# Putting the second layer's first row fetches ahead of its loads in GpSimd's queue

## The chip, the cores and the metric

The kernel runs on one core of one Trainium2 chip. The metric is the device time of one execution in microseconds (us). Before the change it is 1780.5 us, the median of three runs (1777.8 to 1781.71).

## The reference

A graph of 6250 nodes with 128 features, 50,000 undirected edges (so 100,000 directed ones) and one self-loop for each node, sorted by destination. Two residual layers:

```python
h = relu(layernorm(x))
xw = h @ W                                    # layer 0: a normalised graph convolution
x = x + relu(segment_sum(xw[src] * (dinv[src] * dinv[dst])[:, None], dst) + b)
h = relu(layernorm(x))
q, k, v = h[src] @ Wq.T + bq, h[dst] @ Wk.T + bk, h[dst] @ Wv.T + bv   # layer 1: attention over edges
e = exp(clip(einsum("ehd,ehd->eh", q, k) / 4, -10, 10))                # 8 heads of 16
out = segment_sum(e / (segment_sum(e, src)[src] + 1e-8) * v, src) + h
x = x + layernorm(out) * gamma + beta
```

## The kernel before

Nodes lie in 49 blocks of 128. Layer 0 (`layer0`) walks over the edges in the order of their destination: GpSimd fetches rows of xw from a table in HBM (`gtab`) with indirect DMAs of 128 rows (`gather`, line 397), TensorE adds them up by destination with one-hot matrices, and `finish0` finishes a block of 128 nodes as soon as its last edge is in. Its results go by SyncE's queue to tables in HBM: `htab`, `xtab`, `owntab` (q of each node), `kvtab` (k and v, float32), `qtab` (q as three bfloat16 parts), and, for the first 18 blocks alone, `kvptab` (k and v as three bfloat16 parts). Beside this work the kernel sorts the edges for layer 1: each block of 128 source nodes gets J = 20 tiles of 128 edge places. The first 9 tiles (`CELLS`) hold edges whose other end is in the first 18 blocks (two blocks a tile), the remaining 11 (`FAR`) hold the others in ascending order of that end. `unpack` writes the row numbers to `idx1`, and `rows_of` the lane numbers to `lrow` and `drow`. `flags` adds up checks that all hold, and only then the fast path `layer1` is taken (a branch on `self.flag`, line 1552); else `general` computes everything in another way.

Layer 1 (`layer1`) goes through the 49 blocks in five steps of four tiles each, in the order of tiles [8..11], [0..3], [12..15], [4..7], [16..19]. `fetch` gets k and v of the edges' far ends. For tiles from 9 on, GpSimd gathers rows of `kvtab` into a buffer `kv` (nine of them). For tiles under 9, TensorE multiplies one-hot matrices `ohD` with `kvp`, the copy of `kvptab` that is kept in SBUF for the whole layer: 18 blocks, 3456 KB. The one-hot matrices `ohT` and `ohD` are made by VectorE from the rows `lr` and `dr`, and q of the edges comes from `qb`. `load` brings lr, dr and qb of a block, those of block 0 by GpSimd's queue and the others by SyncE's. `weigh` (two steps later) makes the attention weights, `gather_up` (four steps later) sums up. Every eight blocks, `own_edges` loads hs, x, qo and kvo by SyncE's queue and works out the self-loops.

The order within an engine's queue is the program's order of issue with some freedom for a scheduler that looks at dependences; GpSimd's queue keeps the order written in the source. A buffer of layer 1 that lies where layer 0 had buffers waits until layer 0 has let go of them. GpSimd's queue at the seam between the layers holds, in this order: the last gathers of `gtab`, the read of the flag, the load of kvp (line 978), the loads of lr, dr and qb (lines 1004, 1007, 1009), and the gathers of layer 1.

Of the kernel before, what the change touches and what calls it, by code (L numbers as in the profile page):

```python
# [7 lines left out]
F32 = mybir.dt.float32  # L8
# [6 lines left out]
OP = mybir.AluOpType  # L15
# [6 lines left out]
P = 128  # L22
D = 128
# [5 lines left out]
PB = 18  # L29
CELLS = -(-PB // 2)  # L30
FAR = 11
J = CELLS + FAR
BANK0 = 10
G1 = 4
# [5 lines left out]
CW = -(-P // CN)  # L40
CQ = 4
CR = 8
CL = 8
RUN = 128
SEG = 4
# [7 lines left out]
class Kernel:  # L53
    def __init__(self, ctx, tc, x, srcp, dstp, srct, dstt, bases, firsts, wins, w0, b0, wq, bq, wk, bk, wv, bv,
                 gamma, beta, out, E):
        self.ctx, self.tc, self.nc = ctx, tc, tc.nc
        self.x, self.srcp, self.dstp, self.srct, self.dstt = x, srcp, dstp, srct, dstt
        self.bases, self.firsts, self.wins = bases, firsts, wins
        self.w0, self.b0, self.gamma, self.beta, self.out, self.E = w0, b0, gamma, beta, out, E
        self.qkv = ((wq, bq), (wk, bk), (wv, bv))  # L60
        self.N = x.shape[0]
        self.NB = -(-self.N // P)
        self.NP = self.NB * P
        self.LAST = self.N - (self.NB - 1) * P
        self.EC = -(-E // P)
        self.ER = -(-self.EC // P) * P
        self.NR = -(-E // self.ER)
        self.NG0 = -(-self.EC // G0)
        self.ET = self.NG0 * G0
        self.NT1 = self.NB * J  # L70
        assert self.N <= 8192 and self.EC <= 1024 and self.ER <= 1024 and self.ER % SEG == 0
        assert PB < self.NB <= 49 and BANK0 * self.NB <= 512 and (J - BANK0) * self.NB <= 512

        self.NODE0 = (PC - 1) * P
        self.GA = int(PC * P * E / self.N - 4.5 * (PC * P * (E / self.N - 1)) ** 0.5) // (P * G0)

        self.done_at = {}
        for b in range(PC, self.NB):
            last = b + 1 == self.NB
            self.done_at[b] = self.NG0 - 1 if last else min(self.NG0 - 1, -(-(b + 1) * P * E // (self.N * P * G0)) + 1)  # L80
        self.NW = PC // CQ
        assert PC % CQ == 0 and CN * self.NB * 2 <= 512


# [103 lines left out]
    def head(self):  # L188
        nc, tc, const, NB, NP, N, ER = self.nc, self.tc, self.const, self.NB, self.NP, self.N, self.ER
        d_i = self.rows["dst"]  # L190
        self.flag = const.tile([1, 1], I32, name="flag")

        self.bad = const.tile([P, 7], F32, name="bad")
        nc.vector.memset(self.bad, 0.0)
        self.dinv = const.tile([P, NB], F32, name="dinv")
        self.gtab = self.dram.tile([NP, D], F32, name="gtab")
# [2 lines left out]
        with self.first_c:  # L199
# [3 lines left out]
            bad = self.bad  # L203
# [5 lines left out]
            for g, n in groups(NB, 8):  # L209
                st = hw.tile([P, 8, nc.vector.BN_STATS_DIM], F32, name="st0")  # L210
                for b in range(g, g + n):
# [5 lines left out]
                                               op0=OP.mult, op1=OP.mult)  # L217
# [183 lines left out]
    def layer0(self):  # L401
# [19 lines left out]
        with ExitStack() as l0c:  # L421
# [248 lines left out]
            def unpack():  # L670
                vi = big("vi", I32, "big0", NB * J).rearrange("p (a b) -> p a b", b=J)
                for h, f0, f1 in ((0, 0, BANK0), (1, BANK0, J)):
                    v = pp[:, h, :(f1 - f0) * NB].rearrange("p (j b) -> p b j", b=NB)
                    nc.vector.tensor_scalar(vi[:, :, f0:f1], v, 1024.0, None, op0=OP.mult)
                bv = big("bv", F32, "big1", NB * J).rearrange("p (a b) -> p a b", b=J)
                nc.vector.tensor_scalar(bv, vi, 0.0, None, op0=OP.is_gt, op1=OP.add, accum_out=self.bad[:, 5:6])
                ai = ti(NB * J).rearrange("p (a b) -> p a b", b=J)
                nc.vector.tensor_scalar(ai, vi, 10, None, op0=OP.arith_shift_right)
                bi = bv.bitcast(I32)
                nc.vector.tensor_scalar(bi, vi, 1023, None, op0=OP.bitwise_and)  # L680
                nc.vector.tensor_scalar(idx1, ai, 7, 10, op0=OP.bitwise_and, op1=OP.logical_shift_left)
                nc.vector.tensor_tensor(idx1, idx1, bi, op=OP.bitwise_or)
                nc.vector.tensor_scalar(ai, ai, 3, None, op0=OP.arith_shift_right)
                loc = big("loc", F32, "big2", NB * J).rearrange("p (a b) -> p a b", b=J)
                nc.vector.tensor_scalar(loc, ai, -1.0, None, op0=OP.add)
                r["loc"] = loc.rearrange("p a b -> p (a b)")

                r["rel"] = bv.rearrange("p a b -> p (a b)")[:, :NB * CELLS]
                rel = r["rel"].rearrange("p (a b) -> p a b", b=CELLS)
                nc.vector.scalar_tensor_tensor(rel, self.slot_f[:, None, :CELLS].to_broadcast([P, NB, CELLS]),  # L690
                                               -2.0 * P, idx1[:, :, :CELLS], op0=OP.mult, op1=OP.add)


            def flags():
                p5, k = bank()
                nc.tensor.matmul(p5[:1, :7], self.onef, self.bad, start=True, stop=True)
                want = l0k.tile([1, 7], F32, name="want")
                nc.vector.memset(want, 0.0)
                nc.vector.memset(want[:, 1:4], float(N))
                nc.vector.memset(want[:, 5:6], float(E - N))  # L700
                sums = l0k.tile([1, 7], F32, name="sums")
                nc.vector.tensor_tensor(sums, p5[:1, :7], want, op=OP.not_equal)
                let_go(k)
                fails = l0k.tile([1, 5], F32, name="fails")
                nc.vector.tensor_reduce(fails[:, 0:1], sums, axis=AX.X, op=OP.add)
                bf = l0k.tile([1, self.NG0 + 1], F32, name="bf")
                nc.vector.tensor_copy(bf, base_i)

                wide = l0k.tile([1, self.NG0 - GA], F32, name="wide")
                nc.vector.tensor_sub(wide, bf[:, GA + 1:], bf[:, GA:self.NG0])  # L710
                nc.vector.tensor_scalar(wide, wide, float(WIN - 1), None, op0=OP.is_gt, op1=OP.add,
                                        accum_out=fails[:, 1:2])

                nc.vector.tensor_scalar(fails[:, 3:4], bf[:, GA:GA + 1], float(PC * P), None, op0=OP.is_ge)
                nc.vector.tensor_scalar(fails[:, 4:5], bf[:, GA:GA + 1], float(NODE0), None, op0=OP.is_lt)
                late = l0k.tile([1, NB], F32, name="late")
                nc.vector.memset(late, 0.0)
                for b, at in self.done_at.items():
                    if at + 1 < self.NG0:
                        nc.vector.tensor_scalar(late[:, b:b + 1], bf[:, at + 1:at + 2], float((b + 1) * P), None,  # L720
                                                op0=OP.is_lt)
                nc.vector.tensor_reduce(fails[:, 2:3], late, axis=AX.X, op=OP.add)
                total = l0k.tile([1, 1], F32, name="total")
                nc.vector.tensor_reduce(total, fails, axis=AX.X, op=OP.add)
                nc.vector.tensor_scalar(self.flag, total, 0.0, None, op0=OP.is_equal)
# [240 lines left out]
    def layer1(self):  # L966
# [7 lines left out]
        with ExitStack() as l1c:  # L974
            l1k = l1c.enter_context(tc.tile_pool(name="l1k", bufs=1))
            kvp = l1k.tile([P, PB, 3, 2 * D], BF16, name="kvp")

            nc.gpsimd.dma_start(kvp.rearrange("p b c f -> p b (c f)"),
                                self.kvptab.rearrange("(b p) f -> p b f", p=P))
            l1 = l1c.enter_context(tc.tile_pool(name="l1", bufs=2))  # L980
            pqp = l1c.enter_context(tc.tile_pool(name="pqp", bufs=3, space=PSUM))
            kvps = l1c.enter_context(tc.tile_pool(name="kvps", bufs=2, space=PSUM))
# [18 lines left out]
            def load(b, by=nc.sync):  # L1001
                lr = l1.tile([P, J * P], BF16, name="lr", bufs=3)
                src = self.lrow[b * J:(b + 1) * J, :]
                by.dma_start(lr, bass.AP(tensor=src.tensor, offset=src.offset, ap=[[0, P], [1, J * P]]))
                dr = l1.tile([P, CELLS * P], BF16, name="dr", bufs=2)
                src = self.drow[b * CELLS:(b + 1) * CELLS, :]
                by.dma_start(dr, bass.AP(tensor=src.tensor, offset=src.offset, ap=[[0, P], [1, CELLS * P]]))
                qb = l1.tile([P, 3 * D], BF16, name="qb", bufs=3)
                by.dma_start(qb, qtab_v[:, b, :])
                blocks[b] = [lr, qb, dr]  # L1010


            def fetch(b, k):
                if k == 0 and b + 1 < NB:
# [7 lines left out]
                nc.vector.tensor_scalar(ohT[:, :n * P], lr[:, j0 * P:(j0 + n) * P], pid[:, 0:1], None,  # L1022
                                        op0=OP.is_equal)
                if m < n:
                    kv = l1.tile([P, G1, 2 * D], F32, name="kv", bufs=9)
                    for i in range(m, n):
                        self.gather(kv[:, i, :], self.kvtab, idx1, b * J + tiles[i])
                else:
                    kv = l1.tile([P, G1, 2 * D], F32, name="kvn", bufs=5)
                if m:  # L1030
# [86 lines left out]
                                     mine[:, :cn, D:, None].to_broadcast([P, cn, H, HD]))  # L1117

            own, ends = iter(()), {}
            load(0, nc.gpsimd)  # L1120
            for i in range(len(units) + 4):
                if i < len(units):
# [480 lines left out]
```

## Time and profile before

| what | value |
|---|---|
| median of three runs | 1780.5 us (1777.8 to 1781.71) |
| profiled execution | 2244.92 us, span 2243.1 us |
| busy: TensorE, its weight loads, VectorE | 1672.5, 1427.7, 1512.1 us |
| busy: ScalarE, GpSimd | 967.6, 1143.1 us |
| gathers of `gtab` in layer 0 | 567, 1064 ns each on GpSimd |
| gathers of `kvtab` in layer 1 | 539, 983 ns each on GpSimd |
| GpSimd's DMA queue (q0) | 45264 packets, 112.89 MB |
| SyncE's DMA queue (q1) | 116391 packets, 106.65 MB |
| kvp load | one DMA of 3456 KB |

The profile is of one execution, which was longer than the undisturbed ones; durations are taken from it, and the sum is set against its own time. PE is TensorE, PEld its weight load, DVE VectorE, ACT ScalarE, POOL GpSimd; SPq, POOLq are the queues' DMA issues. In the timeline a line has the start in us, the duration in us, engine, source line, operation, what is written and read, how many merged, and in brackets the idle time of the engine before it with what ended it. In the windows, each engine has its busy time in the stretch.

### The profile page before, as it was taken

How to read it: one execution, taken by the hardware profiler on the slowest of the kernel's cores; microseconds unless marked ns; L12 is line 12 of the kernel's file. 1: busy time of each engine (PE TensorE's matmuls, PEld its weight loads, DVE VectorE, ACT ScalarE, POOL GpSimd, SP SyncE). 2: the span in 40 equal slices, each digit the busy share in tenths (PEclk: the TensorE clock that was granted, in tenths of full speed). 3: DMA queues.
4: the chain of work that ended last, by engine and by line, in shares of the span. 5: the costliest groups of instructions: out<-in, count | busy, mean ns of one | idle time of the engine just before them, and what ended most of it. 6: DMA issues, size and time to landing. Idle time of an engine off the chain costs nothing.

```text
span 2243.1 us, 41246 instructions
## 1 busy us (share of the span) xinstructions
PE 1672.5 (75%) x14772; PEld 1427.7 (64%) x14772; DVE 1512.1 (67%) x4504; ACT 967.6 (43%) x2499; POOL 1143.1 (51%) x1124
## 2 busy tenths in 40 slices
PE   4334687777678888887428888787988888888786
PEld 4333576666566677555317777686877777777676
DVE  7821498768748888998227668566767567556667
ACT  6641544423347767775103334233334334333333
POOL 0565523444647667777465555454555453544540
PEclk9556698888775556998559999888888888999898
DMA  4411222222222222222475335434435333432430
GB/s 93 108 49 48 70 70 77 81 72 73 76 69 71 61 63 64 65 64 64 134 243 162 115 123 156 125 122 149 135 115 164 108 119 107 145 105 95 141 105 13
DMA packets 168217, 225.46 MB, mean 101 GB/s; under 512 B 30026, under 2 KB 127803, under 8 KB 168003
## 3 DMA queue, kind: packets, MB, share of 16 engines
q0 software_dynamic: 45264, 112.89, 17.0%
q1 hardware_dynamic: 116391, 106.65, 15.3%
q10 hardware_dynamic: 6348, 3.20, 0.7%
q8 instruction: 118, 1.93, 0.4%
q14 instruction: 96, 0.79, 0.1%
HBM read 191.42 MB, written 31.20 MB: 99 GB/s over the span
## 4 chain that ended last, share of the span: by engine, by line
PE 58%; issue 15%; DVE 11%; ACT 8%; another core or an unknown queue 3%; DMA 2%; POOL 1%; SPq 1%; DVEq 0%; ACTq 0%; POOLq 0%
PE pk L1040 14%; PE po L1079 11%; PE pq L1048 8%; PE cb L797 7%; PE ps L956 5%; PE pp L658 5%; ACT ola L643 3%; PE ot L1052 3%; PE cb L782 1%; PE ps_f L892 1%; ACT counts L785 1%; DVE oh_tau L645 1%; DVE win_oh L771 1%; POOL gt L397 1%
## 5 line engine op out<-in xcount | busy, mean ns | idle before, releaser
L397 POOL DMA_INDIRECT gt<-gtab,idx x567 | 603.5, 1064 | 484.3 <-issue 140.2
L397 POOL DMA_INDIRECT kv<-kvtab,idx x539 | 530.1, 983 | 526.7 <-issue 141.5
L1040 PE MATMUL pk<-kvp,ohD 128*128 128x256 bf16 x2646 | 368.0, 290 | 77.8 <-issue 67.7
L1040 PEld LDWEIGHTS <-ohD 128*128 128x128 bf16 x2646 | 271.0, 104 | 147.1 <-issue 104.3
L643 ACT ACTIVATE ola<-ol,a_f 128x128 f16<-128x128 f16 x624 | 270.2, 519 | 57.5 <-DVE ol L624 37.7
L1048 PE MATMUL pq<-qb,ohT 128*128 128x128 bf16 x2940 | 237.8, 231 | 57.9 <-issue 57.5
L1054 ACT COPY oh<-ot 128x512 f32<-128x512 f32 x245 | 142.6, 583 | 263.9 <-PE pk L1040 90.3
L956 PE MATMUL ps<-oh,gt 128*128 128x64 f32 x1134 | 214.1, 344 | 56.2 <-DVE acc L938 25.2
L1048 PEld LDWEIGHTS <-ohT 128*128 128x128 bf16 x2940 | 204.9, 104 | 79.8 <-issue 71.3
L956 PEld LDWEIGHTS ps<-oh,gt 128*128 128x128 f32 x1134 | 201.4, 261 | 65.5 <-issue 34.9
L797 PE MATMUL cb<-xwp,counts 128*128 128x128 bf16 x2352 | 192.5, 253 | 51.5 <-issue 39.5
L797 PEld LDWEIGHTS <-counts 128*128 128x128 bf16 x2352 | 185.9, 155 | 60.9 <-issue 48.1
L1060 DVE TENSOR_TENSOR pr<-pq,kv 128x512 f32<-128x512 f32 x147 | 101.0, 687 | 173.9 <-DMA kv<-kvtab,idx 66.0
L658 PE MATMUL pp<-oh_tau,ol 128*128 128x49 f16 (+5 forms) x916 | 192.0, 265 | 28.2 <-DVE ol L626 16.3
L785 ACT CAST counts<-cb 128x490 bf16<-128x490 f32 x208 | 113.7, 572 | 173.5 <-PE cb L782 111.2
L645 DVE TENSOR_SCALAR oh_tau<-slot,code 128x98 f16<-128x98 f16 (+5 forms) x831 | 175.5, 271 | 16.2 <-PE pp L658 13.8
L1062 DVE TENSOR_REDUCE att<-pr 128x32 f32<-128x512 f32 x245 | 165.2, 675 | 4.2 <-ACT wv__19893 L1068 1.9
L658 PE MATMUL pp<-oh_tau,ola 128*128 128x49 f16 (+5 forms) x688 | 148.5, 259 | 17.8 <-issue 1.6
L782 PE MATMUL cb<-win_oh,win_ol 128*128 128x245 f16 x416 | 87.1, 300 | 96.9 <-ACT counts L785 35.2
L658 PEld LDWEIGHTS <-ol 128*128 128x128 f16 x916 | 131.0, 155 | 38.3 <-DVE ol L626 22.2
L1066 ACT ACTIVATE ex<-att 128x32 f32<-128x32 f32 x245 | 56.3, 230 | 222.9 <-DVE att L1064 184.7
L1043 ACT COPY kvn<-pk 128x512 f32<-128x512 f32 x196 | 107.9, 578 | 89.9 <-PE pk L1040 29.2
(1281 smaller groups left out, 2905.6 us busy)
## 6 DMA issues: line engine op xcount, KB each, us to landing
lr<-lrow SPq DMA_DIRECT2D x48, 640.0 KB
dr<-drow SPq DMA_DIRECT2D x48, 288.0 KB
gt<-gtab,idx POOLq DMA_INDIRECT x567
kv<-kvtab,idx POOLq DMA_INDIRECT x539
kvtab<-kvout SPq DMA_DIRECT2D x49, 128.0 KB
kvo<-kvtab SPq DMA_DIRECT2D x6, 1024.0 KB
qtab<-qp SPq DMA_DIRECT2D x49, 96.0 KB
qb<-qtab SPq DMA_DIRECT2D x48, 96.0 KB
```

The source lines that it names most:

```text
L397: self.nc.gpsimd.indirect_dma_start(out=to, out_offset=None, in_=table, in_offset=bass.IndirectOffsetOnAxis(ap=idx[:, t:t + 1], axis=0))
L643: nc.scalar.activation(ola, r["ol"][:, 0, :, t % PT], AF.Copy, scale=r["a"][:, t:t + 1])
L645: nc.vector.tensor_scalar(oh[:, :(hi + 1 - lo) * NB], self.slot16[:, lo * NB:(hi + 1) * NB], r["code"][:, t:t + 1], None, op0=OP.is_equal)
L658: nc.tensor.matmul(pp[:, h, (x0 - f0) * NB:(x1 - f0) * NB], o, oh[:, (x0 - lo) * NB:(x1 - lo) * NB], start=False, stop=t == EC - 1, skip_g ...
L785: nc.scalar.copy(self.counts[:, c0:c0 + 2 * CN, :].rearrange("p n b -> p (n b)"), cb[:, :2 * CN * NB])
L797: nc.tensor.matmul(prods[b][:, :D], self.counts[:, :P, k], self.xwp[:, k, x, :], start=(k, x) == (0, 0), stop=(k, x) == (NB - 1, 2))
L956: nc.tensor.matmul(ps, gt[:, j, :], oh[:, j, :], start=(j == 0), stop=(j == n - 1))
L1040: nc.tensor.matmul(pk[:, i - c, :], ohD[:, h, i * P:(i + 1) * P], kvp[:, 2 * tiles[i] + h, x, :], start=(h, x) == mine[0], stop=(h, x) == ...
L1048: nc.tensor.matmul(pq[:, i * D:(i + 1) * D], left, qb[:, x * D:(x + 1) * D], start=(x == 0), stop=(x == 2))
L1054: nc.scalar.copy(oh[:, :n, :], ot[:, :n, :])
L1062: nc.vector.tensor_reduce(att[:, :n * H], pr[:, :n, :].rearrange("p g (h d) -> p (g h) d", h=H), axis=AX.X, op=OP.add)
L1079: nc.tensor.matmul(po, oh[:, i, :], wv_[:, i, :], start=(k == 0 and i == 0), stop=(k == len(steps) - 1 and i == n - 1))
```

## The change

In `layer1`, a function `far_rows` does the gathers of one step. Those of block 0 for the two steps that end in tiles 9 to 16 are issued ahead of everything else on GpSimd's queue (a dictionary `early`), then come the load of kvp and those of lr, dr and qb. Block 0's gathers of the first eight far tiles (9 to 16) read `kvtab[:self.SOON]` in place of the whole table. A new column of `bad` counts row numbers of these tiles that are not under `SOON`; if there is one, the general path is taken.

```diff
+SOON = 8
...
+        low = PB * P + SOON * P * self.N / ((self.E - self.N) / self.N * P)
+        self.SOON = min(self.NB - 1, int(low + 5 * SOON ** 0.5 * P ** 0.5 * self.N / ((self.E - self.N) / self.N * P)) // P + 1) * P
...
-        self.bad = const.tile([P, 7], F32, name="bad")
+        self.bad = const.tile([P, 8], F32, name="bad")
...
+                soon = l0k.tile([P, SOON], F32, name="soon")
+                nc.vector.tensor_scalar(soon, idx1[:, 0, CELLS:CELLS + SOON], float(self.SOON), None, op0=OP.is_ge,
+                                        op1=OP.add, accum_out=self.bad[:, 7:8])
...
-                nc.tensor.matmul(p5[:1, :7], self.onef, self.bad, start=True, stop=True)
+                nc.tensor.matmul(p5[:1, :8], self.onef, self.bad, start=True, stop=True)
...
             kvp = l1k.tile([P, PB, 3, 2 * D], BF16, name="kvp")
-
-            nc.gpsimd.dma_start(kvp.rearrange("p b c f -> p b (c f)"),
-                                self.kvptab.rearrange("(b p) f -> p b f", p=P))
...
+            soon = self.kvtab[:self.SOON, :]
+
+            def far_rows(b, k):
+                kv = l1.tile([P, G1, 2 * D], F32, name="kv", bufs=9)
+                for i, j in enumerate(steps[k]):
+                    if j >= CELLS:
+                        self.gather(kv[:, i, :], soon if b == 0 and j < CELLS + SOON else self.kvtab, idx1, b * J + j)
+                return kv
...
-                    kv = l1.tile([P, G1, 2 * D], F32, name="kv", bufs=9)
-                    for i in range(m, n):
-                        self.gather(kv[:, i, :], self.kvtab, idx1, b * J + tiles[i])
+                    kv = early.pop((b, k), None) or far_rows(b, k)
...
             own, ends = iter(()), {}
+
+            early = {(0, k): far_rows(0, k) for k, s in enumerate(steps) if CELLS <= s[-1] < CELLS + SOON}
+            nc.gpsimd.dma_start(kvp.rearrange("p b c f -> p b (c f)"),
+                                self.kvptab.rearrange("(b p) f -> p b f", p=P))
             load(0, nc.gpsimd)
```

More of the change, by code (lines that the diff above doesn't have):

```diff
@@ L695, in flags @@
                 p5, k = bank()
-                nc.tensor.matmul(p5[:1, :7], self.onef, self.bad, start=True, stop=True)
-                want = l0k.tile([1, 7], F32, name="want")
+                nc.tensor.matmul(p5[:1, :8], self.onef, self.bad, start=True, stop=True)
+                want = l0k.tile([1, 8], F32, name="want")
                 nc.vector.memset(want, 0.0)
@@ L700, in flags @@
                 nc.vector.memset(want[:, 5:6], float(E - N))
-                sums = l0k.tile([1, 7], F32, name="sums")
-                nc.vector.tensor_tensor(sums, p5[:1, :7], want, op=OP.not_equal)
+                sums = l0k.tile([1, 8], F32, name="sums")
+                nc.vector.tensor_tensor(sums, p5[:1, :8], want, op=OP.not_equal)
                 let_go(k)
```

## The prediction

> **What bounds the kernel now.** Start with the page's busy table: TensorE is busy for 75% of the span and VectorE for 67%, so neither layer has a single full engine. But the change touches only the seam between the two layers, so the table decides nothing here. The windows by stage show the seam: from 1120 to 1145 us TensorE does nothing at all while the DMA engines are full.
>
> ```profile
> 1100.00:1105.00 5.00, 3.71 (x13) 2.91 (x14) 2.28 (x10) 1.89 (x6) 0.71 (x1) 0.50 0.74 224
> 1105.00:1110.00 5.00, 2.44 (x12) 1.39 (x12) 3.39 (x16) 2.62 (x8) 0.00 (x0) 0.84 1.03 400
> 1110.00:1115.00 5.00, 2.41 (x5) 0.69 (x4) 1.77 (x7) 1.15 (x5) 0.00 (x0) 0.50 0.87 295
> 1115.00:1120.00 5.00, 2.44 (x4) 0.83 (x4) 0.76 (x4) 1.92 (x6) 0.00 (x0) 0.50 0.25 75
> ...
> 1125.00:1130.00 5.00, 0.00 (x0) 0.00 (x0) 0.00 (x0) 0.00 (x0) 3.27 (x5) 0.50 1.07 333
> 1130.00:1135.00 5.00, 0.00 (x0) 0.00 (x0) 0.00 (x0) 0.00 (x0) 3.78 (x5) 0.50 1.05 330
> ```
>
> Read from left: stretch, its length, then PE, PEld, DVE, ACT, POOL busy, clock, DMA share, GB/s. Next the timeline of GpSimd's queue, which the change reorders:
>
> ```profile
> 1095.22 0.94 POOL L397 DMA_INDIRECT gt<-gtab,idx  x1 [0.30 <-issue]
> 1099.43 1.28 POOL L978 DMA_DIRECT2D kvp<-kvptab  x1 [3.26 <-DVE acc L938]
> 1122.57 0.57 POOL L1004 DMA_DIRECT2D lr<-lrow  x1 [21.86 <-DMA qtab<-qp]
> 1123.65 0.54 POOL L1007 DMA_DIRECT2D dr<-drow  x1 [0.51 <-issue]
> 1124.75 0.54 POOL L1009 DMA_DIRECT2D qb<-qtab  x1 [0.56 <-issue]
> 1126.10 1.02 POOL L397 DMA_INDIRECT kv<-kvtab,idx  x1 [0.81 <-issue]
> 1127.42 0.98 POOL L397 DMA_INDIRECT kv<-kvtab,idx  x1 [0.30 <-issue]
> ```
>
> The 3456 KB kvp load goes out at 1099.43, **21 us before layer 0 has ended**: it fills the 224 to 400 GB/s stretch above and is out of the way by about 1115. Only lr waits (21.86 us) for layer 0's last write, qtab of block 48. Then the whole timeline from 1119 on, for what starts layer 1:
>
> ```profile
> 1124.49 2.54 SPq L1103 DMA_DIRECT2D kvo<-kvtab  x1
> ...
> 1140.32 1.22 DVE L1105 TENSOR_TENSOR qo<-qo,kvo 128x1024 f32<-128x1024 f32 x1 [20.04 <-DMA hs<-htab]
> ...
> 1144.67 1.23 DVE L1115 TENSOR_TENSOR mine<-kvo,mine 128x1024 f32<-128x1024 f32 x1 [1.65 <-issue]
> 1145.82 0.61 DVE L1022 TENSOR_SCALAR ohT<-lr,pid 128x512 bf16<-128x512 bf16 x2
> ...
> 1146.79 1.46 PE L1040 MATMUL pk<-kvp,ohD 128*128 128x256 bf16 x6
> ```
>
> VectorE's first layer-1 instruction needs kvo, which SyncE's queue loads after hs, x and qo; its own-edge work takes 1140.32 to 1145.9, and ohT follows at once. **So kvo's landing starts layer 1**, not the gathers: three of the gathers have been issued by 1129.7, 16 us before they can be of use.
>
> **What the Trainium skill says.** "DMA: Bandwidth & Descriptors", section "Issuing engines are not separate DMA queues": transfers of all issuing engines run on the same 16 DMA engines. The trace agrees: with both queues loaded the share is 1.05 and the rate stays at 330 GB/s. Same page, "Queues, rings and completion order": a DMA engine takes turns between queues packet by packet, so a queue with bigger packets gets more. The trace agrees: page part 3 gives q0 (GpSimd) 2.5 KB a packet (112.89 MB / 45264) and q1 (SyncE) 0.92 KB, and beside kvp the kvtab write issued at 1104.63 holds the chain for 7.53 us, where the last qtab write takes 1.61.
>
> **The change, part by part.** All times are on the profiled execution (2244.9 us, span 2243.1), which is 26% longer than the median of 1780.5. Differences made of DMA bytes I carry over as they are.
>
> 1. *The check* (one VectorE instruction on 128x8; one more column in the flag sums). The nearest rows are tiny VectorE operations of 0.15 to 0.18 us in this stretch. It stands among the unpack operations, which are on the chain. Cost 0.2 us, bounds 0 and 0.3.
>
> 2. *The moved gathers don't start early.* In the built program's order the first moved gather carries the waits that kvp and lr had together: same counts, up to qtab, kvtab and owntab of block 48. Its kv buffer lies in memory that layer 0 holds to its end. Reading only the first rows (the formula gives 47 blocks, not 44: the access has 6016 rows) takes no wait away. kvp, lr, dr and qb are queued behind it. So GpSimd stands until about 1122 and then issues seven gathers (steps [8..11], of which 9 to 11, and [12..15]), 1.25 us each (0.95 and 0.30 gap): 8.75 us. The eighth restricted gather, tile 16, keeps its place.
>
> 3. *kvp loses its cover.* Issued at 1122.57 - 1.2 (parts 1 and 4) + 8.75 = 1130.1, against 1099.4. 3456 KB are 3.54 MB. Before, 1100 to 1115 moved 5 x (224 + 400 + 295) KB = 4.6 MB, most of it kvp: about 280 GB/s for it, 12.6 us. It lands at about 1144, and lr, dr and qb (1024 KB, 1.05 MB) behind it at about 1147.5. The pk matmuls and ohT can't start before that. Bounds: 10 us for kvp at 360 GB/s; 21 us at half of 335.
>
> 4. *Layer 0's tail is relieved.* In the tail kvout waits for a write slowed by kvp: it starts at 1113.95, though its matmul ended at 1112.54. Relief 1.4 us. Bounds: none, and 6 us: the chain shows 7.53 + 1.69 us of DMA there and two ordinary landings are 3.2. The upper one holds if TensorE's steps are shorter without the profiler, so that the write becomes the only limit.
>
> 5. *kvo gets late.* SyncE's loads up to kvo are 2560 KB = 2.62 MB, and took 1122.05 to 1140.3. Now GpSimd's queue offers only gathers (131 KB per 1.25 us, 105 GB/s) for the first 8.75 us, which leaves 230 GB/s for some 7.5 us of them: 1.75 MB. The remaining 0.87 MB run beside kvp. SyncE's writes got about 0.7 MB through from 1104.6 to 1113.9 beside kvp, 75 GB/s: 11.6 us. kvo lands at 1130.5 + 11.6 = 1142, own-edge work (5.5 us) ends at 1147.5, when lr lands too. ohT starts at 1147.5 to 1149 against 1145.82. Two more ohT now stand ahead of the first ohD, 0.7 us.
>
> 6. *Later gathers*: the same eleven DMAs in another order, plus kvp's 1.8 us: no loss of order, buffers or gathers later. SyncE now issues qo of the second group ahead of lr for block 1, so that load waits for VectorE's first product, about 1143, instead of 1135.45; needed after five steps, it should arrive in time. Zero, up to 3 us.
>
> Sum, tail relief and check already inside: 1148.3 - 1145.8 = 2.5 us, plus 0.7, plus 0.8 for a share of part 6: **4 us later**. Ends: kvo not delayed and full relief, 4.5 us earlier; kvo starved until kvp, lr and the gathers queued meanwhile have drained (to about 1153), 12.5 us later.
>
> **The rivals.**
> *A, absorbed.* From 1152 to 1172 TensorE issues a matmul only every 1.4 to 2.5 us with "issue" as the reason, until GpSimd's run of gathers ends at 1168.07. If that run sets the restart, a start 3 us later hides in it; the run itself ends 36 gathers later as before, 0.6 us shifted. Time 1781. Against it: the profiler may make this stretch, since 465 us of the execution are its own.
> *B, faster.* The tail relief is near its 6 us because the last blocks' writes are the limit, and exceeds the 2 to 3 us by which ohT starts later after the release. Net 4.5 us: 1776. It decides from a relief over about 7 - 2 us; the profile shows only 1.4.
> *C, fully exposed.* SyncE's queue gets nearly nothing while kvp, lr and ten further gathers (1.3 MB) drain: 12.5 us, 1793.
> *D, it does what it says*: the gathers go at about 1110, when block 46's kvtab write (issued 1108.44) has landed. The waits in the program speak against it; kvp would still be 20 us later, and nothing waits for those gathers: 1780.
>
> **How the numbers follow.** About 0.2% (3.6 us) is what a measurement of this kernel can tell from no change; the three runs shown spread over 3.9. My forecast, 3 to 8 us slower through kvp's lost cover: 0.45, time 1784.5, its own range 1783.5 to 1788.5. A 0.22, B 0.18, C 0.12, D 0.03. Of the forecast a sixth falls under 3.6 us. Slower: 0.38 + 0.12 + 0.03 of A = 0.53. Same: 0.07 + 0.18 + 0.03 = 0.28. Faster: B and a rest of A, 0.19. The range reaches from B's 1776 to C's 1793.
>
> **What would show it.** Right: kvp's load at about 1130 behind seven gathers that start at about 1121, the first gather waiting for a last write of layer 0; the stretch 1100 to 1115 at well under 200 GB/s; kvout's wait there gone; ohT and pk two to five us later after the last qtab write than the 25.5 us of before. Wrong: kv gathers before 1115, or kvo landing within 17 us of the release, or a last qtab write earlier by over 4 us.

## The result and the profile after

The changed kernel takes **1796.48 us** (median of five runs, 1792.95 to 1797.62). The kernel before, run beside it, takes 1781.71 us (1777.8 to 1787.85). The ratio is **1.0061, with a 95% interval of 1.0043 to 1.0079**, so 7.7 to 14.1 us slower; the two medians alone differ by 14.8 us. The profiled execution of the changed kernel took 1797.62 us, span 1795.7.

One fact is needed to read the numbers below: executions of these kernels come near 1780 us on some chips and near 2270 us on others, so ratios compare kernels on one chip only. The profile of before that the prediction used (2244.9 us) was of the second kind. For a comparison with the profile after I took a new one of the unchanged kernel (experiment 9, called **before again** from here on; 1783.5 us, span 1781.5). In both of these profiles the last write of layer 0 (qtab of block 48) is issued at nearly the same time, 973.92 us before and 974.31 us after. I count from this moment and write +11 for 11 us after it. To the end of the span it is 807.6 us before and 821.4 us after: **13.8 us lost, all of it in layer 1**. That is the difference of two single executions, near the upper end of the 7.7 to 14.1 us above.

The windows of the seam, the kernel after (stretch, length, busy PE, PEld, DVE, ACT, POOL, then clock, DMA share, GB/s):

```profile
960.00:965.00 5.00, 3.08 (x7) 1.36 (x7) 2.61 (x11) 1.83 (x6) 0.00 (x0) 0.50 0.12 40
965.00:970.00 5.00, 2.88 (x6) 1.12 (x6) 2.22 (x9) 1.89 (x7) 0.00 (x0) 0.50 0.31 98
970.00:975.00 5.00, 2.22 (x4) 0.65 (x3) 0.58 (x2) 1.21 (x4) 0.00 (x0) 0.50 0.23 74
...
995.00:1000.00 5.00, 0.00 (x0) 0.00 (x0) 0.28 (x1) 0.00 (x0) 0.00 (x0) 0.50 1.03 362
...
1010.00:1015.00 5.00, 3.94 (x51) 3.55 (x49) 0.00 (x0) 0.32 (x1) 3.78 (x5) 1.00 1.04 374
```

The same stretches in the profile of before again:

```profile
960.00:965.00 5.00, 3.00 (x6) 1.17 (x7) 2.54 (x11) 1.86 (x6) 0.56 (x1) 0.50 0.73 210
965.00:970.00 5.00, 2.75 (x6) 0.95 (x5) 1.57 (x7) 1.86 (x6) 0.00 (x0) 0.50 1.03 406
970.00:975.00 5.00, 1.04 (x3) 0.03 (x1) 0.58 (x2) 0.94 (x3) 0.00 (x0) 0.50 0.90 316
...
995.00:1000.00 5.00, 0.31 (x3) 0.24 (x3) 3.32 (x8) 1.54 (x2) 4.09 (x4) 0.50 1.05 378
...
1010.00:1015.00 5.00, 5.00 (x68) 4.80 (x67) 4.95 (x10) 2.94 (x9) 3.80 (x4) 1.00 0.78 267
```

In the last 15 us of layer 0 the DMA engines moved 5 x (210 + 406 + 316) KB = 4.7 MB before and 1.1 MB after. That is kvp (3.54 MB), gone from here. From 980 to 1010 us the engines are full in both kernels, at 311 to 378 GB/s, and what was not moved before has to go through there. From 1010 to 1015 VectorE does nothing at all in the kernel after; before, it is busy for 4.95 of the 5 us.

GpSimd's queue in the timeline of after (start, duration, engine, line, operation, in brackets the idle time ahead and what ended it):

```profile
976.75 0.94 POOL L401 DMA_INDIRECT kv<-kvtab,idx  x1 [19.65 <-DMA qtab<-qp]
...
985.20 1.30 POOL L1133 DMA_DIRECT2D kvp<-kvptab  x1
986.48 0.60 POOL L1008 DMA_DIRECT2D lr<-lrow  x1
...
1002.65 0.94 POOL L401 DMA_INDIRECT kv<-kvtab,idx  x1 [8.38 <-DMA kvp<-kvptab]
```

And of before again:

```profile
959.27 1.28 POOL L978 DMA_DIRECT2D kvp<-kvptab  x1 [3.91 <-issue]
976.33 0.57 POOL L1004 DMA_DIRECT2D lr<-lrow  x1 [15.77 <-DMA qtab<-qp]
```

The first early gather goes at 976.75, when lr went before: it waits for the same last write. Nothing is earlier, kvp is issued 25.5 us later (+10.9 against -14.6) and lr 9.8 us later (+12.2 against +2.4). What that does shows on VectorE, whose timeline in the kernel after is:

```profile
989.69 1.23 DVE L1116 TENSOR_TENSOR qo<-qo,kvo 128x1024 f32<-128x1024 f32 x1 [15.41 <-DMA kvo<-kvtab]
...
1004.26 1.29 DVE L1035 TENSOR_SCALAR ohT<-lr,pid 128x512 bf16<-128x512 bf16 x4 [8.98 <-DMA lr<-lrow]
1005.48 1.59 DVE L1044 TENSOR_SCALAR ohD<-dr,pid 128x128 bf16<-128x128 bf16 x6
1016.04 0.42 DVE L1044 TENSOR_SCALAR ohD<-dr,pid 128x128 bf16<-128x128 bf16 x2 [8.97 <-DMA dr<-drow]
1016.37 0.68 DVE L1071 TENSOR_TENSOR pr<-pq,kv 128x512 f32<-128x512 f32 x1
```

and in before again:

```profile
993.63 1.23 DVE L1105 TENSOR_TENSOR qo<-qo,kvo 128x1024 f32<-128x1024 f32 x1 [20.28 <-DMA kv<-kvtab,idx]
...
999.13 0.61 DVE L1022 TENSOR_SCALAR ohT<-lr,pid 128x512 bf16<-128x512 bf16 x2
...
1001.03 1.00 DVE L1033 TENSOR_SCALAR ohD<-dr,pid 128x512 bf16<-128x512 bf16 x4
1002.94 0.69 DVE L1060 TENSOR_TENSOR pr<-pq,kv 128x512 f32<-128x512 f32 x1 [0.92 <-ACT kv L1043]
```

The bracket on qo names gathers before and kvo after; both stand for a first product that needs kvo. **Two waits of 9 us stand in the kernel after where there is none before.** The first is for lr, in line behind kvp. The second is for a dr: block 0 has three steps with tiles under 9 and so six ohD, and the seventh and eighth are block 1's, which VectorE has ahead of the first pr in both kernels. (pr is the product of q and k in `weigh`, att its sums by head: the first work of a step after `fetch`.) So the first pr comes at +42.1 against +29.0: 13.0 us. The fifth att is at +54.0 against +41.0, the 60th at +226.9 against +213.1, the 200th at +659.1 against +645.3: nothing is given back after that.

### The profile page after: what moved, and what is told of

The parts are those of the page before. It is cut to its first block, busy times and chain, and to the rows that moved or that the text cites. A ratio compares the mean times of both kernels' runs of the same rounds, so it can differ in the third digit from the quotient of the medians.

```text
span 1795.7 us, 41240 instructions
## 1 busy us (share of the span) xinstructions
PE 1505.0 (84%) x14772; PEld 1327.0 (74%) x14772; DVE 1502.2 (84%) x4506; ACT 963.3 (54%) x2499; POOL 1163.8 (65%) x1124
## 4 chain that ended last, share of the span: by engine, by line
PE 50%; DVE 21%; ACT 10%; DMA 7%; issue 6%; POOL 4%; SPq 1%; DVEq 0%; ACTq 0%; POOLq 0%
PE pk L1051 13%; PE po L1090 11%; PE pq L1059 7%; PE cb L804 5%; ACT ola L647 5%; PE ps L963 4%; POOL gt L401 3%; DVE oh_tau L649 3%; PE pp L662 3%; DMA gt<-gtab,idx 3%; PE ot L1063 2%; DVE scan L558 2%; PE ps_f L899 2%; DMA kvo<-kvtab 2%; DVE win_oh L778 1%
## 5 line engine op out<-in xcount | busy, mean ns | idle before, releaser
L401 POOL DMA_INDIRECT kv<-kvtab,idx x539 | 545.1, 1011 | 231.7 <-issue 125.2
L1051 PE MATMUL pk<-kvp,ohD 128*128 128x256 bf16 x2646 | 315.1, 274 | 10.4 <-ACT kvn L1054 10.4
L1051 PEld LDWEIGHTS <-ohD 128*128 128x128 bf16 x2646 | 259.2, 98 | 41.2 <-issue 11.1
L963 PEld LDWEIGHTS ps<-oh,gt 128*128 128x128 f32 x1134 | 194.8, 247 | 96.9 <-DMA gt<-gtab,idx 36.7
L1059 PE MATMUL pq<-qb,ohT 128*128 128x128 bf16 x2940 | 205.5, 219 | 0.2 <-DVE pr L1071 0.2
L662 PE MATMUL pp<-oh_tau,ol 128*128 128x49 f16 (+5 forms) x916 | 182.4, 257 | 15.6 <-DVE ol L630 13.2
L1059 PEld LDWEIGHTS <-ohT 128*128 128x128 bf16 x2940 | 185.9, 98 | 5.7 <-issue 0.3
L804 PEld LDWEIGHTS <-counts 128*128 128x128 bf16 x2352 | 170.5, 154 | 7.4 <-ACT counts L792 6.2
L804 PE MATMUL cb<-xwp,counts 128*128 128x128 bf16 x2352 | 171.3, 242 | 4.0 <-ACT counts L792 4.0
L662 PE MATMUL pp<-oh_tau,ola 128*128 128x49 f16 (+5 forms) x688 | 143.8, 252 | 19.2 <-ACT ola L647 2.3
L1054 ACT COPY kvn<-pk 128x512 f32<-128x512 f32 x196 | 110.6, 575 | 38.0 <-PE pk L1051 37.6
L662 PEld LDWEIGHTS <-ola 128*128 128x128 f16 x688 | 72.7, 114 | 74.1 <-ACT ola L647 68.8
```

The source lines that it names most:

```text
L401: self.nc.gpsimd.indirect_dma_start(out=to, out_offset=None, in_=table, in_offset=bass.IndirectOffsetOnAxis(ap=idx[:, t:t + 1], axis=0))
L662: nc.tensor.matmul(pp[:, h, (x0 - f0) * NB:(x1 - f0) * NB], o, oh[:, (x0 - lo) * NB:(x1 - lo) * NB], start=False, stop=t == EC - 1, skip_g ...
L804: nc.tensor.matmul(prods[b][:, :D], self.counts[:, :P, k], self.xwp[:, k, x, :], start=(k, x) == (0, 0), stop=(k, x) == (NB - 1, 2))
L963: nc.tensor.matmul(ps, gt[:, j, :], oh[:, j, :], start=(j == 0), stop=(j == n - 1))
L1051: nc.tensor.matmul(pk[:, i - c, :], ohD[:, h, i * P:(i + 1) * P], kvp[:, 2 * tiles[i] + h, x, :], start=(h, x) == mine[0], stop=(h, x) == ...
L1059: nc.tensor.matmul(pq[:, i * D:(i + 1) * D], left, qb[:, x * D:(x + 1) * D], start=(x == 0), stop=(x == 2))
```

## The experiments

The experiments use the terms of the prediction. A ratio is to the kernel before on the same chip. Experiments 1 to 8 and 12 ran on chips near 2270 us, 9 to 11 on one near 1780 us.

**1. The kernel before near 2270 us.** No edit.

> The kernel before, unchanged, for a second profile: the first one's execution took 2245 us against a median of 1780.5, the changed kernel's own took 1797.6. Both theories expect an execution near 1780 us with kvp issued some 20 us before layer 0's last write and landed before it; theory 1 (kvp's lost cover) expects the first ohT about 20 to 22 us after the issue of the last qtab write, against 29.95 us in the changed kernel; the rival (order of the queues, not kvp's bytes) expects the same start to within 3 us and a loss in the steps after it.

It took 2279.31 us, not near 1780 us as expected, with ohT at +24.8 and the first pr at +35.8, against +25.5 and +49.3 in the first profile of before. So the crawl of TensorE behind the start (a matmul only every 1.4 to 2.5 us, rival A's cover) comes with that kind of execution, and the first pr moves by 13.5 us from one execution to the next; the cause of the crawl stays open.

**2, 6 and 12. The kvp load first again**, the early gathers, the restricted rows and the condition kept:

```diff
 (the changed kernel)
             kvp = l1k.tile([P, PB, 3, 2 * D], BF16, name="kvp")
+            nc.gpsimd.dma_start(kvp.rearrange("p b c f -> p b (c f)"), ...)
...
             early = {(0, k): far_rows(0, k) for k, s in enumerate(steps) if CELLS <= s[-1] < CELLS + SOON}
-            nc.gpsimd.dma_start(kvp.rearrange("p b c f -> p b (c f)"), ...)
             load(0, nc.gpsimd)
```

> The changed kernel with one part undone: kvp's load stands where it stood before, ahead of everything in GpSimd's queue; the seven early gathers still stand ahead of lr, dr and qb. Theory 1 (kvp's 3.54 MB moved from beside layer 0's tail into the loaded stretch, some 10 us at 340 GB/s): back to the time of before, ratio 0.999 to 1.002. Rival (lr, dr and qb late behind seven gathers, and SyncE's loads in another order): most of the loss stays, ratio 1.004 to 1.006.

> The changed kernel with kvp's load back ahead of the early gathers, a second time, on the same chip as the changed kernel. Theory 1: at or under the time of before, ratio 0.996 to 1.001. Rival (queue order, with lr behind seven gathers): 1.003 or more.

> The changed kernel with one thing undone: the kvp load is issued where the kernel before has it, ahead of the early gathers. SyncE's own order of loads stays the changed one (the second group's qo ahead of block 1's lr and dr). The question is asked for executions near 1780 us, where the changed kernel has its fifth att 53.4 us after the last qtab write and the kernel before 40.5, and where half of kvp loaded early still left 48.9, most of it in a wait of ohD for block 1's dr. Theory (kvp's bytes behind the release delay both lr and block 1's dr): ohT at +21 to +26, dr of block 1 issued at about +21.5 and no wait for it above 3 us, fifth att at +40 to +43, end within 3 us of the kernel before measured from the same write, ratio 0.998 to 1.001. Rival (the order of SyncE's loads alone makes block 1's dr late, whatever kvp does): ohD waits 6 to 10 us for dr, fifth att at +45 to +49, ratio 1.002 to 1.004. Should the executions come near 2270 us, the start can differ by 14 us without a trace in the time, and the ratio says nothing on this; then only the issue of dr and the wait for it can be read.

The ratios are 0.9971 [0.9946, 0.9995], 0.9997 [0.9972, 1.0023] and 0.9989 [0.9964, 1.0014]: no loss left, and the first is just below the range that was expected. In all three ohT is at +21.0 to +21.3 and the first pr at +32.2 to +32.6; the changed kernel on such a chip (experiment 5, the same chip as 6) has +30.0 and +42.4. SyncE issues its loads in the same order in all four. **So kvp's place alone moves the first pr by 10 us.** The third run was to tell what SyncE's changed order of loads does by itself. Its VectorE timeline:

```profile
1155.42 1.28 DVE L1037 TENSOR_SCALAR ohT<-lr,pid 128x512 bf16<-128x512 bf16 x4
1156.62 1.59 DVE L1046 TENSOR_SCALAR ohD<-dr,pid 128x128 bf16<-128x128 bf16 x6
1166.26 0.42 DVE L1046 TENSOR_SCALAR ohD<-dr,pid 128x128 bf16<-128x128 bf16 x2 [8.05 <-issue]
```

Here the rival was right about the wait: with kvp out of the way, block 1's dr, issued at +20.6, is still waited for. (The bracket says "issue", but the instruction is the one that waits for dr in the kernel after.) It costs less than its 8 us, because ohT is 4 us earlier than before. The first pr at +32.2 stands against +29.0 in before again, so the order of SyncE's loads is worth **about 3 us of the 13**. That compares two chips, so it is an estimate; the changed kernel's first pr is at +42.1 on one and +42.4 on the other. What it does to the whole time near 1780 us wasn't measured.

**3. Only kvp moved**: in the kernel before, its load is put behind block 0's lr, dr and qb. No early gathers and no condition.

```diff
 (the kernel before)
-            nc.gpsimd.dma_start(kvp.rearrange("p b c f -> p b (c f)"), ...)
...
             load(0, nc.gpsimd)
+            nc.gpsimd.dma_start(kvp.rearrange("p b c f -> p b (c f)"), ...)
```

> The kernel before with one thing done: kvp's load moved behind lr, dr and qb, no early gathers and no check. Theory 1: the cover is lost in the same way, 7 to 12 us, ratio 1.004 to 1.007. Rival: lr isn't late here, so ratio 0.999 to 1.003.

The ratio is 1.0033 [1.0011, 1.0055], as large as that of the whole change on such a chip (next). But the program as built differs in more than kvp's place: SyncE issues block 1's lr, dr and qb at +2.2 to +3.3, ahead of qo and kvo, and kvo at +9.4 (before: +4.2). lr, now ahead, is in at +11.0, but VectorE then waits 15.07 us for kvo (its product at +32.8), and the first pr is at +37.3. The third att, at +42.5, is still ahead of experiment 1 on the same chip (+57.0), the fifth, at +70.0, is behind it (+61.8). What stands in line beside or behind kvp pays, lr and dr in the changed kernel, kvo here; how much of the loss comes from SyncE's order is not shown.

**5. The changed kernel again**, no edit.

> The changed kernel itself, beside the kernel before on the chip of this call, since the two profiles that I compared came from executions of 2245 and 1798 us. Theory 1 (kvp's lost cover, a number of bytes moved into a loaded stretch) expects the loss in us to be much the same on any chip, 6 to 14 us, so a ratio of 1.003 to 1.008. If the 1.0061 of the first comparison came from the chips and not from the change, 0.999 to 1.002.

2279.16 us, ratio 1.0034 [1.0008, 1.006]; ohT at +30.0, as on the other chip. But here the loss may take another path. GpSimd's first gather behind kvp waits 9.44 us for it, and GpSimd's run of gathers, which goes on until the kv buffers are used up, ends about that much later. The gather after the run, here and in experiment 12 (the run ends where the bracketed wait begins):

```profile
1204.27 0.95 POOL L401 DMA_INDIRECT kv<-kvtab,idx  x1 [9.01 <-DVE wv__14922 L1085]
1194.03 0.95 POOL L401 DMA_INDIRECT kv<-kvtab,idx  x1 [8.68 <-DVE wv__14922 L1087]
```

That is +60.0 against +51.0, and the third att is at +66.1 against +56.8. In all ten profiles of executions near 2270 us TensorE's crawl ends 2.5 to 4.3 us after this run, which ends between +46.9 and +61.7, while ohT comes anywhere from +11.0 to +30.0. **So near 2270 us the loss goes with the end of GpSimd's run, not with ohT**, as rival A has it. No run here moved the end of the run alone, and the DMA engines' backlog is longer in the same kernels, so this stays a correlation.

**4. The condition and the restricted rows alone**, no DMA moved (in the changed kernel, `early = {}` and kvp first):

> The check alone: one VectorE instruction and one more column in the sums, the first eight far tiles of block 0 read the first 6016 rows, and no DMA is moved. Theory 1 and the rival: 0.2 us, ratio 0.999 to 1.001. A third reading, that the check costs several us on VectorE's chain, expects 1.003 or more.

Ratio 0.9981 [0.9955, 1.0007], ohT at +25.7 as before: no cost that can be measured.

**7. The changed kernel without the restriction** (the early gathers read the whole `kvtab`):

```diff
 (the changed kernel)
-                        self.gather(kv[:, i, :], soon if b == 0 and j < CELLS + SOON else self.kvtab, idx1, b * J + j)
+                        self.gather(kv[:, i, :], self.kvtab, idx1, b * J + j)
```

> The changed kernel with the eight restricted gathers reading the whole kvtab; the check stays. My reading of the waits is that the restriction takes no wait away, because the kv buffers come free only with layer 0's last write: the same time as the changed kernel to within 2 us. If the restriction does let the gathers go early, this one is slower than the changed kernel by 2 to 6 us, and its first gather is issued later after the last qtab write.

The first early gather is at +2.5, kvp at +10.9 and ohT at +30.0, as in the changed kernel; ratio 1.0019 [0.9989, 1.0048]. **Reading only the first rows buys nothing**: with or without it the gathers go when layer 0 is over.

**9. Before again near 1780 us** and **10. half of kvp covered.** The first is shown above. In the second, nine of kvp's 18 blocks are loaded ahead of the early gathers and nine behind:

```diff
 (the changed kernel)
+            def part(b0, b1):
+                nc.gpsimd.dma_start(kvp[:, b0:b1]..., self.kvptab[b0 * P:b1 * P, :]...)
+            part(0, PB // 2)
...
-            nc.gpsimd.dma_start(kvp.rearrange("p b c f -> p b (c f)"), ...)
+            part(PB // 2, PB)
```

> The kernel before once more, for a profile beside those of this call. Read by the seam: first ohT about 25 us and the fifth att about 61 us after the issue of the last qtab write if the execution is near 2270 us, as in all profiles of kernels with kvp first so far; about 42 us for the fifth att if it is near 1780 us, since the changed kernel had 53.4 there in an execution of 1798 us and the loss was 10.9.

> The changed kernel with half of kvp (its first 9 blocks, 1728 KB) loaded at the old place, ahead of everything, and the other half behind the early gathers. If the loss goes with the bytes that lie behind layer 0's end, half of it stays: first ohT at 25 to 26 us after the last qtab write (21 with all of kvp early, 30 with none), and, in an execution near 2270 us, the fifth att at 65 to 70 us (61 with all early, 76 with none). If it goes with the order alone (lr behind some kvp load), it stays as in the changed kernel: 30 and 76 us.

Before took 1783.5 us and the half 1795.33 us (one execution each, so that the difference in time is a sample and not a measured ratio). From the last qtab write to the end the half takes 816.5 us, against 807.6 and 821.4: 8.9 us lost. Its VectorE timeline:

```profile
1001.33 1.29 DVE L1040 TENSOR_SCALAR ohT<-lr,pid 128x512 bf16<-128x512 bf16 x4 [3.26 <-DMA lr<-lrow]
...
1014.17 0.42 DVE L1049 TENSOR_SCALAR ohD<-dr,pid 128x128 bf16<-128x128 bf16 x2 [10.03 <-DMA dr<-drow]
```

The wait for lr shrinks from 8.98 to 3.26 us, that for dr doesn't. The first pr, at +37.6, lies about midway between that of all kvp late (+42.1) and of all kvp early (+32.2 in experiment 12, on a chip near 2270 us), as a cost that goes by kvp's bytes would have it.

**8 and 11. Own edges later.** If SyncE's early loads compete with those that start layer 1, hold the former back. In the kernel before, the own edges of the first two groups come in blocks 2 and 10, by one-column copies on ScalarE that their loads wait for; the later groups start two blocks later too. Experiment 11 also has six kv buffers in place of nine.

```diff
 (the kernel before)
-            def own_edges(c0):
+            def own_edges(c0, after):
...
+                def held(t):
+                    if c0 <= CL:
+                        nc.scalar.copy(t[:, 0, 0:1], after[:, 0, 0:1])
+                    return t
-                hs = l1.tile([P, CL, D], F32, name="hs1")
+                hs = held(l1.tile([P, CL, D], F32, name="hs1"))
... (x1, qo and kvo likewise)
+            owns = {min(c + 2, NB - 1): c for c in range(0, NB, CL)}
...
-                    if units[i][0] % CL == 0 and units[i][1] == 0:
-                        own = own_edges(units[i][0])
+                    if units[i][0] in owns and units[i][1] == 0:
+                        own = own_edges(owns[units[i][0]], state[units[i]][1])
```

> The kernel before with the loads and the work of the first two groups' own edges held back until block 2 (block 10), by four one-column ScalarE copies for each of the two groups that the loads must wait for; every other group starts two blocks later too. kvp stays at its old place. If kvo's landing and the own-edge work are what starts layer 1 in the kernel before (the step on which my sum stands), ohT starts 10 to 15 us after the last qtab write in place of 25, and the kernel is 6 to 14 us faster, ratio 0.993 to 0.997. If the start is set by lr or by the gathers, ratio 0.998 to 1.002.

> The kernel before with the own edges held back as in the earlier run, and six kv buffers in place of nine, so that GpSimd's first run of gathers is 23 and not 35 long. In executions near 2270 us all kernels with kvp first had the third att at 56 to 57 us, whether ohT came at 11 or at 25. If the end of GpSimd's unbroken run sets that time, it moves to about 40 us and the kernel gets 6 to 14 us faster (ratio 0.994 to 0.998) unless the shorter lookahead costs it later. If a fixed backlog of other loads sets it, it stays at 55 or more, ratio 0.999 to 1.003.

In experiment 8 ohT comes at +11.5, 14 us earlier than before, yet the third att, traced in its longest execution (2296.38 us), is at +57.3 (before: +56.6), and the ratio is 1.0011 [0.9979, 1.0044]: near 2270 us the crawl behind the start swallows the gain. Experiment 11 was to test whether the end of GpSimd's run sets the end of the crawl, but it came on a chip near 1780 us, where there is no crawl. It has ohT at +11.7 and the fifth att at +28.1, 12.9 us ahead of before, and a ratio of **0.9986 [0.9974, 0.9998]** (1783.26 against 1785.11 us). That is faster than the kernel before, by little, and two things were changed in it. Most of the lead is given back between the tenth att (+42.1 against +57.4) and the 100th (+334.6 against +337.4). Part of it shows in its list of waits from 993 to 1045 us (engine and line, waited for, sum, times, longest):

```profile
DVE qo L1110 <- DMA kvo<-kvtab: 7.0, 1, 7.0
```

The loads that were held back are waited for later. The rest of the way back wasn't taken apart.

## Why the prediction was right and wrong

The direction was right and so were its first links; the size was not. It gave 4 us. By the ratio 7.7 to 14.1 us came, around the 12.5 us of the range's slow end; the median of the five runs lies 3.5 us beyond that end (1793 us), and the two profiles differ by 13.8.

- **The moved gathers don't start early (2): right.** The first waits 19.65 us for qtab's last write and goes at +2.4; experiment 7 shows that the restriction changes nothing. Rival D is out.
- **kvp loses its cover (3): right in place, short in time.** Issued at +10.9, as worked out. GpSimd's first gather that waits for it goes 17.4 us after its issue, where the prediction had about 14 (1130.1 to 1144). Its rate was no worse than the 280 GB/s assumed. From 975 to 990 us GpSimd's queue moved 0.92 MB, which is the seven gathers (7 x 131 KB) and nothing of kvp; from 990 to 1002 us the two queues moved (packets, MB, share of the engines' time; q0 is GpSimd's, q1 SyncE's):

```profile
q0 software_dynamic: 815, 3.70, 85.6%
q1 hardware_dynamic: 1216, 0.61, 19.6%
```

  That is 308 GB/s for GpSimd's queue. What was missed is that kvp, issued at 985.2, moved only from about 990, with the gathers of its own queue ahead of it. ohT came at +30.0, at the late end of the predicted +28.4 to +29.9 (1147.5 to 1149, with the last qtab write at 1119.1).
- **kvo gets late (5): wrong.** It was in by +15.4, 4.3 us *earlier* than before, which the prediction had named as a sign against it. By 990 us SyncE's queue had moved 3.16 MB since 975, more than its 2.62 MB up to kvo, and kvp had not begun. The starved remainder of 11.6 us at 75 GB/s did not exist. Rival C's starvation was real, 0.61 MB in 12 us, but kvo was already in: it fell on SyncE's loads for block 1. That C's time (1793) is nearly right is luck, since it was worked out for kvo.
- **SyncE's loads for block 1 (6): the step that failed, as a term that was mis-sized.** "Needed after five steps, it should arrive in time. Zero, up to 3 us" became a wait of 8.97 us. It is there with kvp early too (8.05 us in experiment 12), so it goes with the order of SyncE's loads and of VectorE's work; kvp adds about 1 us to it and delays what comes ahead of it. Two things were missed. VectorE's order has block 1's ohD ahead of block 0's first pr, so dr is needed at once; that was to be read in the timeline of before, where eight ohD go by before pr. And the loads that wait behind qo for VectorE's product then issue while kvp fills the engines. SyncE's queue in the timeline of after:

```profile
982.07 2.62 SPq L1110 DMA_DIRECT2D x<-xtab  x1
992.20 0.36 SPq L1112 DMA_DIRECT2D qo<-owntab  x1
992.60 9.03 SPq L1008 DMA_DIRECT2D lr<-lrow  x2
1001.68 1.14 SPq L1011 DMA_DIRECT2D dr<-drow  x1
```

  and of before again:

```profile
985.18 3.81 SPq L1099 DMA_DIRECT2D x<-xtab  x1
989.03 4.09 SPq L1004 DMA_DIRECT2D lr<-lrow  x1
993.16 0.43 SPq L1007 DMA_DIRECT2D dr<-drow  x1
```

  SyncE stands from 984.7 to 992.2 for qo's buffer, then spends 9.03 us on issuing two lr, and dr goes out at +27.4 against +19.2. The sum by measurement: ohT 4.7 us later (+30.0 against +25.2), and from ohT to the first pr 12.1 us in place of 3.8, so 8.3 more: 13.0 us. Of the 8.3 the prediction had 0.7 + 0.8.
- **The relief of layer 0's tail (4): not there.** The last kvout waits 2.10 us where it waited 2.70, now for TensorE. The last qtab write comes at 973.9 before and 974.3 after. Rival B is out.
- **The check (1): right** within what experiment 4 can tell.
- **"465 us of the execution are the profiler's own" (in rival A): wrong.** Profiled executions take 1783.5 and 1797.62 us where the runs take 1780 and 1796. The crawl was real on that chip, and absent near 1780 us, so nothing absorbs a late start there. The worked numbers for 1780 us should have left it out. And A's run of gathers, "0.6 us shifted", ended 9 us later near 2270 us, because it stood behind kvp (experiment 5).

So the shown cause is kvp's place: of two kernels that differ in it alone, the changed one loses (1.0034) and the one with kvp first doesn't (0.9997 on the same chip, 0.9971 and 0.9989 on two others). This pair was run near 2270 us only. Near 1780 us, where the prediction stands, half of kvp moved first took back 4.5 us of the first pr and 4.9 us of the whole, in one execution each. Experiment 3 fits, but has SyncE's loads in another order too. That SyncE's order adds about 3 us is an estimate.

## What to carry to other kernels

Before moving a small transfer ahead of a large one in a queue, ask what the large one was covered by: here a load that could run under layer 0 was put behind gathers that could not, and it then took its bytes from the loads that start the next stage. Follow every load that is made late to the first instruction that reads it in its engine's own order, not in the loop's order: the reader of block 1's dr stood ahead of block 0's first product. And a view read in one kind of execution is worth checking in another before a stall in it is counted on as cover.

## What the runs showed of the hardware

- Here the queue with the larger packets got most of what the full DMA engines moved. From 990 to 1002 us GpSimd's queue, with kvp in it, moved 3.70 of 4.31 MB, 86%, and SyncE's queue 0.61 MB, 51 GB/s; it spent 9.03 us of this time on issuing two lr. The Trainium skill's page "DMA: Bandwidth & Descriptors", section "Queues, rings and completion order", says that a DMA engine takes turns between queues packet by packet. By the packets of this stretch (4.5 and 0.50 KB) equal turns would give GpSimd's queue 90%; it had 815 packets against 1216, so the turns come near to equal and are not.
- GpSimd's gather at 1002.65 waits 8.38 us for kvp, which it doesn't read. It is the eighth DMA behind kvp on that queue, and the next one waits 0.90 us for lr, its own eighth before. Experiment 3 has the same (9.54 us). So in these programs a slow load holds up the eighth DMA behind it on GpSimd's queue. Near 1780 us no wait of VectorE or TensorE was found behind it; for executions near 2270 us see experiment 5.
- A start that was 14 us earlier (experiment 8) left no trace by the third att near 2270 us, and near 1780 us it lasted to the tenth. What stalls TensorE in the former executions stays open; that the stall ends with GpSimd's run of gathers is all that the profiles show.
